# Two transformer layers on one core: expert rows weighted where they are made, and gathers that add

## The chip, the cores and the metric

The kernel runs on one core of a Trainium2 chip. The core has a matrix engine (TensorE, PE in the profile), three engines for element-wise work (VectorE or DVE, ScalarE or ACT, GpSimd or POOL), and a queue for transfers on SyncE (SP); POOL issues the transfers whose addresses come from a table of indices ("indirect" DMAs). The metric is the device time of one execution in microseconds (us).

## The reference, cut to what matters

The input x has 8 x 256 = 2048 tokens of 512 float32 values. Layer 1 is a linear attention of 32 heads plus, on the same normed input, a mixture of experts; layer 2 is a softmax attention plus a low-rank mixture.

```python
# layer 1
xn = layernorm(x)
x = x + linear_attention(xn) + ffn0(xn)
# ffn0: 2 of 16 experts for each token, and a shared one
def step(y, p):
    w1, b1, w2, b2, w3, b3, ge = p            # ge: this expert's gate of each token (0 if not chosen)
    h = silu(xt @ w1 + b1) * (xt @ w2 + b2)
    return (y + ge[:, None] * (h @ w3 + b3), None)
# layer 2
xn = layernorm(x)
x = x + attention(xn) + ffn1(xn)
# ffn1: 16 of 64 rank-16 factors for each token, gates G
h   = einsum('nd,krd->nkr', xf, A)
out = einsum('nkr,kdr->nd', h * G[:, :, None], B) * 2
```

Each token has two expert rows; the sum over experts is gate 1 x row 1 + gate 2 x row 2.

## The kernel before, in words

*Tiles and chunks.* The tokens form 4 chunks of 512, each of 4 tiles of 128 tokens. Large matrix products are done by a seven-product scheme of the Strassen kind in two-by-two blocks: products p1, p2, p6, p7, p5, p3, p4 go to PSUM banks `ps_a`, `ps_b`, `ps_e`, and the element-wise engines combine them.

*Layer 1.* A plan runs over two halves (of two chunks each), eight groups of four heads, two parts of a group and seven products (L1025). Other work is put between these products in small pieces: `later(after, f)` (L1030) notes a piece with the slot from which it may go, and `slot()` (L1034) runs those that are due after each product. Among them are:

- Routing: `scatter` (L1484 to 1492), 32 times. POOL makes a tile `token` with the token numbers (an iota, L1487) and scatters it by an indirect DMA (L1488) into a table with one line per expert slot. `read_table` (L1494) loads the table back, and `take_table` copies its first column to `whose`, the token of each slot.
- Experts: the class `Expert` (L1040 on), for 36 tiles of 128 slots in this run. Its construction gathers the tokens' rows and the weights (L1051, L1056, both into a tile `xw`: `xe` holds the rows, `we` the weights). `turn` transposes the rows (L1065) and copies them (L1067); `bias` then gathers the bias rows b3 into the same place `xe` (L1071); `up` makes h (L1083 to 1091); `down` multiplies with w3 (L1095), adds `xe` with DVE (L1100, shown at the helper's L103 as `ye`) and stores the row to `yd` in HBM (L1101). `expert(j)` (L1461) puts turn, bias, up and down at slots 10, 11, 14 and 22 after its start.
- At the end of the half: `wrapped_up` (L1564) makes chunk 0 ready for layer 2.

*From the experts' rows to x.* `gather` (L748 to 756) fetches for each tile and each of the two choices n the rows of `yd` by indirect DMA into a buffer `y`; `settle` (L758 to 767) is a DVE step, x = y * gate + x (L763). `finish` (L783) adds the attention's output, x = acc * rms + x (L789).

*The first factor.* `fa` has 14 pieces of 128 x 512 (seven products, two contraction halves). `load_part` (L937) loads pieces 0 to 8 in three calls during layer 1, each call three pieces into a tile that has room for 3.5 of them; `rest`, pieces 9 to 13, is loaded at the start of layer 2 (L1758), behind `wo` and `bo` (L1741, L1742). Piece 9 is the second half of product p5.

*Layer 2.* The chunk loop (L1778 on) does for every chunk i: the first low-rank product (L1806) as two half products, `low_rank(0, fill1)` and `low_rank(2, fill2)`, each by `seven` (L1692); attention in between; then the second product (L1913) and the stores (L1928). `seven` runs the lists `fill[k]` behind product k. Outputs of the first half product are multiplied by the gates on POOL and those of the second on DVE; both write `hg` out of a bank or a copy `cp` and a gate tile `spread_g`, loaded by SP (L920) into one of two buffers named `spread`. Chunk 0's first pair of gate tiles has room of its own. A half product has four outputs, written after p2, p5, p3 and p4; the first and third read one gate tile, the second and fourth the other. `fill2` holds `attended` (L1856): a POOL addition of `bo`, a product with `wo` (L1859) and a DVE addition.

In chunk i the input of chunk i + 1 is made ready: `next_x` loads x (L1772), the eight gathers stand ahead of everything else (L1862 to 1866), the settling steps in `fill1[3]`, `fill1[4]`, `fill2[2]`, `fill2[7]`, for i above 0 the `finish` steps in `fill1[2]` and `fill1[7]`, the norm's statistics in `fill2[7]`, `fill2[5]`, and its scaling in `fill2[3]`, `fill2[4]`. On POOL the parts of the attention's sums are also combined (`combine`, seven additions named `acc`).

*Order.* From the beginning of the chunk loop the instructions of ACT, POOL and DVE stand in the order in which the program gives them. TensorE's and SP's order is chosen by a scheduler. Every engine and SP work through their own queue in order, so an instruction that waits holds up all behind it.

Of the kernel before, what the change touches and what calls it, by code (L numbers as in the profile page):

```python
# [9 lines left out]
FP = mybir.dt.float32  # L10
# [63 lines left out]
def block_kernel(  # L74
# [566 lines left out]
    own_ = const.tile([P, NMT], I32, name="own_")  # L641
    whose = [const.tile([P, n], I32, name=f"whose{n}") for n in (READ, NMT - READ)]

    places = const.tile([P, TOP, NTT], I32, name="places")
# [103 lines left out]
    def gather(i, n, y, ts=range(TPC)):  # L748

        for t in ts:  # L750
            at = i * TPC + t
            nc.gpsimd.indirect_dma_start(
                out=y[:, t, :], out_offset=None, in_=yd[:, :],
                in_offset=bass.IndirectOffsetOnAxis(ap=slots[:, n, at : at + 1], axis=0),
                bounds_check=NSLOT - 1, oob_is_err=False,
            )

    def settle(i, n, x_, y, ts=range(TPC)):  # L758

        for t in ts:  # L760
            gate = slot_gates[:, n, i * TPC + t : i * TPC + t + 1]
            tc.keep_in_program_order(
                nc.vector.scalar_tensor_tensor(  # L763
                    x_[:, t, :], y[:, t, :], gate, x_[:, t, :], ALU.mult, ALU.add
                )
            )
# [160 lines left out]
    def load_fa(t, lo, hi):  # L927

        for n in range(lo, hi):
            p, c = list(WA)[n // 2], n % 2  # L930
            a = dict(
                p1=fa[:, 0], p2=fa[:, 1], p4=fa[:, 2], p7=low[0][:, 0], p5=low[0][:, 1], p6=low[0][:, 2], p3=low[0][:, 3]
            )[p]
            nc.sync.dma_start(out=t[:, n - lo], in_=a[:, bass.ts(c, C)])
            WA[p].append(t[:, n - lo])

    def load_part(n):  # L937

        t = toks.tile([P, 7, S], FP, tag="X", name="fa")
        load_fa(t.rearrange("p b n -> p (b n)")[:, 0 : 3 * C].rearrange("p (c k) -> p c k", c=3), 3 * n, 3 * n + 3)  # L940

# [3 lines left out]
    with in_order, tc.tile_pool(name="attn", bufs=1) as attn:  # L945
# [88 lines left out]
        def slot():  # L1034

            now[0] += 1
            n = 0
            while pieces and pieces[0][0] <= now[0] and n < (2 if len(pieces) > 12 else 1):
                f = pieces.pop(0)[2]
                f()  # L1040
                n += getattr(f, "func", f).__name__ not in ("add_a", "bias_sum", "silu", "bias", "gate", "fill_tile", "read_table", "take_table", "scatter", "load_sum", "sums1", "sums2", "sums3", "sums4", "settle0", "settle1", "out_sum", "load_sums", "store_sum", "combine", "finish", "store", "ranks", "tiles_of", "starts", "owners", "owned", "rows", "slots_of", "end", "placed", "chosen_at", "gated_at")


        class Expert:
# [24 lines left out]
            def bias(self):  # L1069
# [404 lines left out]
        def beyond():  # L1474

            with tc.If(n_used[0] > USUAL):  # L1476
                for j in range(USUAL, NMT):
                    e = Expert(j)
                    e.turn()
                    e.bias()  # L1480
                    e.up()
# [12 lines left out]
        def read_table(n=0):  # L1494
# [10 lines left out]
            def take_table():  # L1505
                tc.keep_in_program_order(
                    nc.vector.tensor_copy(
                        whose[n], rows.bitcast(I32).rearrange("p (j o) -> p j o", o=SAME)[:, :, 0]
                    )
                )  # L1510
                if n == 0:
                    read_table(1)
# [42 lines left out]

        def settled_in(i, x_, y):

            tc.keep_in_program_order(nc.sync.dma_start(out=x_, in_=xs_[i]))
            gathered(i, 0, y, 0)
            later(19, partial(settle, i, 0, x_, y))  # L1560
            gathered(i, 1, y, 20)
            later(39, partial(settle, i, 1, x_, y))

        def wrapped_up():  # L1564

            x_, y = spare8(), spare8()
            settled_in(0, x_, y)
            accs.append(x_)
# [171 lines left out]
    wo_t, bo_t = wob[:, 0, :], wob[:, 1, :]  # L1740
    nc.sync.dma_start(out=wo_t, in_=wo)  # L1741
    nc.sync.dma_start(out=bo_t, in_=bo.to_broadcast([P, C]))  # L1742
    HK = KR // 2
# [34 lines left out]
    for i in range(NCH):  # L1778
# [15 lines left out]
        def low_rank(j, fill):  # L1794
# [8 lines left out]
            def product(bank, w, xx, first):  # L1803
                for n in range(2):
                    for c in range(HC):
                        mm(  # L1806
                            bank[:, bass.ts(n, S)], w[c][:, bass.ts(j + n, P)], xx[:, c, :],
                            start=(first and n == 0 and c == 0), stop=(c == HC - 1),
# [64 lines left out]
        if following:  # L1873
# [156 lines left out]
```

## Time and profile before

| | |
|---|---|
| time, median of 3 runs | 2644.53 us (2644.34 to 2647.04) |
| profiled execution | 2642.12 us, of which span 2640.4 us |
| mean granted TensorE clock | 0.999 |
| TensorE busy | 2612.6 us, 99% |
| DVE busy | 1755.3 us, 66% |
| POOL busy | 1322.1 us, 50% |
| ACT busy | 704.3 us, 27% |
| settling steps (L763), DVE | 32, 27.6 + 10.5 us |
| gathers (L752), POOL | 32, 35.1 us |
| layer 2, chunk loop | from about 2359 us to the end |

A row of a timeline reads: start, time until the last of the row ends, engine, line, operation, output<-inputs, shape, count, and in square brackets the idle time of the engine before it with the instruction that ended it. A row of the waits reads: who waited for whom, total, number of times, longest (us). A row of the stretches reads: length, busy time (and count) of PE, PEld, DVE, ACT and POOL, then the granted TensorE clock, the share of the DMA engines and GB/s. Times are us from the span's start. Many additions share L103, a helper; they are told apart by the names of their tiles.

### The profile page before, as it was taken

The page shows a single profiled execution, that of the slowest core. Times are in us where ns is not written, and L with a number is a line of the kernel's source. Part 1 is how long each engine was busy: PE and PEld are TensorE (multiplying, and loading weights), DVE is VectorE, ACT ScalarE, POOL GpSimd, SP SyncE. Part 2 cuts the span into 40 slices and gives each one's busy share as a digit, 9 for nine tenths or more (in the row PEclk, how much of TensorE's full clock was granted, in tenths as well). Part 3 has the DMA queues.
Part 4 walks back from the last instruction along what each step waited for, and adds up shares of the span by engine and source line. Part 5 has one row for each costly group of instructions (what it writes and reads, how often), then busy time and mean ns, then how long its engine had stood idle before and what let it go on. Part 6 is the DMA issues. An engine that isn't in the chain of part 4 may idle for free. (4 is left out here: it accounts for less than half of the span.)

```text
span 2640.4 us, 38395 instructions
## 1 busy us (share of the span) xinstructions
PE 2612.6 (99%) x14250; PEld 2288.8 (87%) x14250; DVE 1755.3 (66%) x3211; ACT 704.3 (27%) x995; POOL 1322.1 (50%) x1297
## 2 busy tenths in 40 slices
PE   9999999999999999999999999999999999999999
PEld 6588888888888898989889898988989898977777
DVE  6795768686867686757456565656566565756774
ACT  5123232323232323232323122222312232321111
POOL 6756575656565656554534334352433453344411
PEclk9999999999999999999999999999999999999999
DMA  8996868686878777777777676777767686634201
GB/s 318 340 346 248 303 243 306 242 309 241 308 256 295 261 287 259 285 272 273 266 252 272 233 290 210 283 250 265 262 244 273 238 313 227 220 120 148 79 33 60
DMA packets 163117, 655.60 MB, mean 248 GB/s; under 512 B 19776, under 2 KB 22336, under 8 KB 160960
## 3 DMA queue, kind: packets, MB, share of 16 engines
q1 hardware_dynamic: 125504, 496.02, 53.0%
q10 hardware_dynamic: 21456, 95.95, 9.2%
q0 software_dynamic: 15968, 61.13, 6.9%
q8 instruction: 116, 1.90, 0.3%
q14 instruction: 73, 0.60, 0.1%
HBM read 512.13 MB, written 143.78 MB: 248 GB/s over the span
## 5 line engine op out<-in xcount | busy, mean ns | idle before, releaser
L1025 PE MATMUL ps_a<-xt,w 128*128 128x256 f32 x2688 | 712.6, 380 | 4.8 <-DVE c L103 4.7
L1025 PEld LDWEIGHTS ps_a<-xt,w 128*128 128x128 f32 x2688 | 470.1, 191 | 59.8 <-issue 9.3
L103 POOL TENSOR_TENSOR c<-c,r 128x512 f32<-128x512 f32 x256 | 323.2, 1286 | 247.3 <-DVE r L103 245.5
L1222 PE MATMUL ps_sc<-wo,gT 128*128 128x256 f32 x1792 | 422.4, 379 | 0.5 <-PEq L1476 0.5
L1222 PEld LDWEIGHTS ps_sc<-wo,gT 128*128 128x128 f32 x1792 | 334.3, 190 | 45.0 <-issue 2.3
L1025 PE MATMUL ps_e<-xt,w 128*128 128x256 f32 x1344 | 365.4, 381 | 3.7 <-PE ps_a L1025 3.0
L103 POOL TENSOR_TENSOR w<-w 128x512 f32<-128x512 f32 (+1 forms) x243 | 244.5, 1017 | 234.1 <-DVE w L103 194.8
L103 POOL TENSOR_TENSOR sums<-sums,sq 128x256 f32<-128x256 f32 x240 | 179.0, 746 | 313.9 <-ACT sq L1160 303.8
L1025 PEld LDWEIGHTS ps_a<-w,xt 128*128 128x128 f32 x1792 | 270.5, 191 | 23.0
L1025 PE MATMUL ps_a<-w,xt 128*128 128x128 f32 x1792 | 272.2, 274 | 0.0
L1025 PEld LDWEIGHTS ps_e<-xt,w 128*128 128x128 f32 x1344 | 230.2, 191 | 28.1 <-PE ps_a L1025 5.2
L103 DVE TENSOR_TENSOR acc<-ps_sc,acc 128x512 f32<-128x512 f32 x196 | 135.0, 689 | 153.0 <-PE ps_sc L1222 152.5
L1362 ACT COPY cp<-ps_a 128x512 f32<-128x512 f32 x160 | 93.5, 585 | 533.6 <-PE ps_a L1025 515.0
L103 DVE TENSOR_TENSOR cp<-ps_a,c 128x512 f32<-128x512 f32 x288 | 198.0, 687 | 54.1 <-PE ps_a L1025 45.7
L1169 DVE SCALAR_TENSOR_TENSOR gT<-ps_o,nw,c 128x256 f32<-128x256 f32 x256 | 112.1, 479 | 165.8 <-ACT sq L1160 139.0
L1160 ACT ACTIVATE sq<-ps_o 128x512 f32<-128x512 f32 x128 | 76.5, 597 | 485.0 <-PE ps_o L1150 445.7
L103 DVE TENSOR_TENSOR c<-ps_a,c 128x512 f32<-128x512 f32 x224 | 150.8, 684 | 76.8 <-PE ps_a L1025 75.8
L103 DVE TENSOR_TENSOR w<-w 128x256 f32<-128x256 f32 x333 | 179.1, 538 | 18.3 <-POOL w L103 14.5
L1025 PE MATMUL ps_b<-xt,w 128*128 128x256 f32 x672 | 181.9, 380 | 0.0
L103 DVE TENSOR_TENSOR s<-ps_sc,decay 128x384 f32<-128x384 f32 x256 | 141.3, 554 | 59.6 <-PE ps_sc L1137 58.1
L103 POOL TENSOR_TENSOR gT<-gT 128x512 f32<-128x512 f32 x128 | 164.8, 1288 | 5.8 <-DVE gT L1169 3.2
L1149 PE MATMUL ps_o<-s,c 128*128 128x256 f32 x512 | 154.4, 383 | 0.5
(304 smaller groups left out, 4130.1 us busy)
## 6 DMA issues: line engine op xcount, KB each, us to landing
xt<-xc SPq DMA_DIRECT2D x224, 896.0 KB
w<-in_w_att_dram SPq DMA_DIRECT2D x144, 512.0 KB
w<-in_w_att_dram SPq DMA_DIRECT2D x48, 384.0 KB
wo<-in_w_out_dram SPq DMA_DIRECT2D x56, 256.0 KB
decay<-dec SPq DMA_DIRECT2D x32, 384.0 KB
yd<-ye SPq DMA_DIRECT2D x36, 256.0 KB
wos<-wo ACTq DMA_DIRECT2D x32, 256.0 KB
wo<-wos SPq DMA_DIRECT2D x32, 256.0 KB
```

Of the source, the lines that this page charges most:

```text
L103: (eng or nc.vector).tensor_tensor(o, a, b, op)
L1025: mm(o, a, b, start=(first and ty == 0), stop=True, skip_group_check=True)
L1149: mm(po[:, bass.ts(hh, S)], v[:, 0:P], s[:, 0:S], start=True, stop=False)
L1160: nc.scalar.activation(sq, po, AF.Square)
L1169: nc.vector.scalar_tensor_tensor(gT[:, h, :], po[:, bass.ts(h, S)], nw[:, n : n + 1], self.c[:, 2 * h + t, 0:S], ALU.mult, ALU.mult,)
L1222: mm(py[:, bass.ts(t, S)], self.O[l, p][:, hh, bass.ts(t, P)], self.wo[p][:, hh, :], start=(t == 0 and hh == 0), stop=(hh == 1), skip_grou ...
L1362: nc.scalar.copy(c, bank)
```

## The change

1. The gate of a token is scattered with the token's number: POOL copies it into column 1 of `token`, 32 times, and `take_table` also copies that column, to `gate_of`.
2. A new step `weigh`, at slot 20 of an expert, multiplies the bias rows by the gate on ACT, and `down` computes ye = h w3 * gate + xe in one DVE step.
3. The gathers add to x where it lies (`compute_op`); `settle` is gone. They have no bounds check. A tile's second gather comes after its first has landed.
4. In the chunk loop the gathers of choice 0 stand in `fill1[1]` and those of choice 1 in `fill1[5]`. `finish` moves from `fill1[2]`, `fill1[7]` to `fill2[2]`, `fill2[7]`. In POOL's queue of layer 2, a chunk's gathers of choice 1 stand between the second and the third `hg`; the first four gathers of all stand ahead of the last `sums` steps of layer 1's attention.
5. `load_part(0)` and `load_part(1)` load one more half piece each (piece 9, in the room left in their tiles). `rest` has 4 pieces and is loaded ahead of `wo` and `bo`.

```diff
             nc.gpsimd.indirect_dma_start(
                 out=y[:, t, :], out_offset=None, in_=yd[:, :],
                 in_offset=bass.IndirectOffsetOnAxis(ap=slots[:, n, at : at + 1], axis=0),
-                bounds_check=NSLOT - 1, oob_is_err=False,
-            )
-
-    def settle(i, n, x_, y, ts=range(TPC)):
-
-        for t in ts:
-            gate = slot_gates[:, n, i * TPC + t : i * TPC + t + 1]
-            tc.keep_in_program_order(
-                nc.vector.scalar_tensor_tensor(
-                    x_[:, t, :], y[:, t, :], gate, x_[:, t, :], ALU.mult, ALU.add
-                )
+                compute_op=ALU.add,
             )
...
-            WA[p].append(t[:, n - lo])
+            WA[p].append([t[:, n - lo, bass.ts(m, P)] for m in range(4)])
+
+    split = []
...
+        t = toks.tile([P, 7, S], FP, tag="X", name="fa").rearrange("p b n -> p (b n)")
+        load_fa(t[:, 0 : 3 * C].rearrange("p (c k) -> p c k", c=3), 3 * n, 3 * n + 3)
+        if n < 2:
+            rest = t[:, 3 * C :]
+            nc.sync.dma_start(out=rest, in_=low[0][:, 1, C + n * S : C + (n + 1) * S])
+            split.extend(rest[:, bass.ts(m, P)] for m in range(2))
+        else:
+            WA["p5"].append(split)
...
+            def weigh(self):
+
+                j = self.j
+                self.gate = gate_of[j // READ][:, j % READ : j % READ + 1]
+                nc.scalar.activation(self.xe, self.xe, AF.Copy, scale=self.gate)
...
-                add(ye, py, self.xe)
+                nc.vector.scalar_tensor_tensor(ye, py, self.gate, self.xe, ALU.mult, ALU.add)
...
+            later(20, e.weigh)
...
+            nc.gpsimd.tensor_copy(token[:, 1:2].bitcast(FP), slot_gates[:, n, t : t + 1])
...
-        def settled_in(i, x_, y):
+        def settled_in(i, x_):
 
             tc.keep_in_program_order(nc.sync.dma_start(out=x_, in_=xs_[i]))
-            gathered(i, 0, y, 0)
-            later(19, partial(settle, i, 0, x_, y))
-            gathered(i, 1, y, 20)
-            later(39, partial(settle, i, 1, x_, y))
+            for n in range(TOP):
+                gathered(i, n, x_, 10 + 12 * n)
...
-    rest = work.tile([P, 5, C], FP, tag="fa", name="fa", bufs=1)
-    load_fa(rest, 9, 14)
+    rest = work.tile([P, 4, C], FP, tag="fa", name="fa", bufs=1)
+    load_fa(rest, 10, 14)
+    nc.sync.dma_start(out=wo_t, in_=wo)
+    nc.sync.dma_start(out=bo_t, in_=bo.to_broadcast([P, C]))
...
-            following = [next_x(i + 1), spare(), spare()]
-            for n in range(TOP):
-                gather(i + 1, n, following[1 + n])
+            following = [next_x(i + 1)]
...
+            for k, n in ((1, 0), (5, 1)):
+                fill1[k].append(partial(gather, i + 1, n, following[0]))
             if i:
-                for k, ns in ((2, (0, 1)), (7, (2, 3))):
-                    fill1[k].append(lambda ns=ns: finish(i + 1, following[0], ns, tc.keep_in_program_order))
-            for n, fill, k, ts in (
-                (0, fill1, 3, (0, 1)), (0, fill1, 4, (2, 3)), (1, fill2, 2, (0, 1)), (1, fill2, 7, (2, 3)),
-            ):
-                fill[k].append(partial(settle, i + 1, n, following[0], following[1 + n], ts))
+                for ns, k in (((0, 1), 2), ((2, 3), 7)):
+                    fill2[k].append(lambda ns=ns: finish(i + 1, following[0], ns, tc.keep_in_program_order))
```

More of the change, by code (lines that the diff above doesn't have):

```diff
@@ L642, in block_kernel @@
     whose = [const.tile([P, n], I32, name=f"whose{n}") for n in (READ, NMT - READ)]
+    gate_of = [const.tile([P, n], FP, name=f"gate_of{n}") for n in (READ, NMT - READ)]
     places = const.tile([P, TOP, NTT], I32, name="places")
@@ L934, in load_fa @@
             nc.sync.dma_start(out=t[:, n - lo], in_=a[:, bass.ts(c, C)])
-            WA[p].append(t[:, n - lo])
+            WA[p].append([t[:, n - lo, bass.ts(m, P)] for m in range(4)])
+    split = []
     def load_part(n):
-        t = toks.tile([P, 7, S], FP, tag="X", name="fa")
-        load_fa(t.rearrange("p b n -> p (b n)")[:, 0 : 3 * C].rearrange("p (c k) -> p c k", c=3), 3 * n, 3 * n + 3)
+        t = toks.tile([P, 7, S], FP, tag="X", name="fa").rearrange("p b n -> p (b n)")
[6 more added lines that the diff above has]
+            WA["p5"].append(split)
     def spare8():
@@ L1040, in slot @@
                 f()
-                n += getattr(f, "func", f).__name__ not in ("add_a", "bias_sum", "silu", "bias", "gate", "fill_tile", "read_table", "take_table", "scatter", "load_sum", "sums1", "sums2", "sums3", "sums4", "settle0", "settle1", "out_sum", "load_sums", "store_sum", "combine", "finish", "store", "ranks", "tiles_of", "starts", "owners", "owned", "rows", "slots_of", "end", "placed", "chosen_at", "gated_at")
+                n += getattr(f, "func", f).__name__ not in ("add_a", "bias_sum", "silu", "bias", "gate", "fill_tile", "read_table", "take_table", "scatter", "load_sum", "sums1", "sums2", "sums3", "sums4", "settle0", "settle1", "out_sum", "load_sums", "store_sum", "combine", "finish", "store", "ranks", "tiles_of", "starts", "owners", "owned", "rows", "slots_of", "end", "weigh", "placed", "chosen_at", "gated_at")
         class Expert:
@@ L1480, in beyond @@
                     e.bias()
+                    e.weigh()
                     e.up()
@@ L1505, in take_table @@
             def take_table():
[L1506 to L1510, printed above, removed]
+                at = rows.rearrange("p (j o) -> p j o", o=SAME)
+                for o, i in ((whose[n].bitcast(FP), 0), (gate_of[n], 1)):
+                    tc.keep_in_program_order(nc.vector.tensor_copy(o, at[:, :, i]))
                 if n == 0:
@@ L1554, in gathered @@
                 later(after + 2 * t, partial(gather, i, n, y, (t,)))
[L1556 removed]
+        def settled_in(i, x_):
             tc.keep_in_program_order(nc.sync.dma_start(out=x_, in_=xs_[i]))
[L1559 to L1562 removed]
+            for n in range(TOP):
+                gathered(i, n, x_, 10 + 12 * n)
         def wrapped_up():
             x_, y = spare8(), spare8()
[L1567 removed]
+            settled_in(0, x_)
             accs.append(x_)
@@ L1740, in block_kernel @@
     wo_t, bo_t = wob[:, 0, :], wob[:, 1, :]
-    nc.sync.dma_start(out=wo_t, in_=wo)
-    nc.sync.dma_start(out=bo_t, in_=bo.to_broadcast([P, C]))
     HK = KR // 2
@@ L1806, in product @@
                         mm(
-                            bank[:, bass.ts(n, S)], w[c][:, bass.ts(j + n, P)], xx[:, c, :],
+                            bank[:, bass.ts(n, S)], w[c][j + n], xx[:, c, :],
                             start=(first and n == 0 and c == 0), stop=(c == HC - 1),
```

## The prediction

> **What bounds the kernel now.** I read the engine table first, then the chain of waits of TensorE, then the table of stretches around every wait found, then the timelines there.
>
> ```profile
> PE 2612.6 (99%) x14250; PEld 2288.8 (87%) x14250; DVE 1755.3 (66%) x3211; ACT 704.3 (27%) x995; POOL 1322.1 (50%) x1297
> ...
> PE ps_e L1806 <- DVE cp L103: 5.1, 2, 4.1
> ...
> PE ps_a L1806 <- DMA fa<-low: 1.5, 1, 1.5
> PE ps_e L1913 <- DVE hg L103: 1.3, 2, 0.7
> ...
> 2380.00:2390.00 10.00, 6.21 (x23) 3.79 (x21) 9.84 (x12) 0.59 (x1) 9.77 (x7) 1.00 0.92 307
> 2390.00:2400.00 10.00, 9.66 (x45) 8.28 (x46) 9.46 (x18) 1.16 (x3) 7.67 (x8) 0.83 0.55 174
> ```
>
> TensorE is the bound: 2612.6 of 2640.4 us. Saved DVE work is worth only the TensorE waits that it ends. Waits this change can end lie in layer 2: 1.5 on a piece of the first factor, 4.1 and 0.99 on DVE's `cp`, 1.3 on DVE's `hg`. The last two rows show the 4.1 (6.21 of 10 us busy) and its echo: the granted clock is 0.83 in the next 10 us, 0.17 x 10 = 1.7 us of matmul time. All of it is under 10 us. About 0.2% (5.3 us) is what a measurement of this kernel can tell from no change.
>
> Chunk 0, DVE:
>
> ```profile
> 2369.29 5.04 DVE L763 SCALAR_TENSOR_TENSOR spare<-spare,slot_gates 128x512 f32<-128x512 f32 x2
> 2374.86 2.41 DVE L763 SCALAR_TENSOR_TENSOR spare<-spare,slot_gates 128x512 f32<-128x512 f32 x2
> 2380.10 1.31 DVE L103 TENSOR_TENSOR hg<-cp,spread_g 128x512 f32<-128x512 f32 x1 [2.22 <-DMA spread_g<-gd]
> 2381.93 2.83 DVE L763 SCALAR_TENSOR_TENSOR spare<-spare,slot_gates 128x512 f32<-128x512 f32 x2
> 2385.28 2.82 DVE L763 SCALAR_TENSOR_TENSOR spare<-spare,slot_gates 128x512 f32<-128x512 f32 x2
> 2389.63 0.66 DVE L103 TENSOR_TENSOR cp<-ps_e,cp 128x512 f32<-128x512 f32 x1
> ```
>
> The last row releases the waiting matmul; two pairs of settling steps stand between it and the `hg` of 2380.10. Now the same product in chunk 1, on POOL, the SP queue, DVE and TensorE:
>
> ```profile
> 2445.56 1.71 POOL L103 TENSOR_TENSOR hg<-cp,spread_g 128x512 f32<-128x512 f32 x1 [3.91 <-DVE cp L103]
> 2447.51 1.44 POOL L103 TENSOR_TENSOR hg<-cp,spread_g 128x512 f32<-128x512 f32 x1 [0.24 <-ACT cp L1817]
> ...
> 2448.97 4.17 SPq L920 DMA_DIRECT2D spread_g<-gd  x4
> ...
> 2454.01 1.36 DVE L103 TENSOR_TENSOR hg<-cp,spread_g 128x512 f32<-128x512 f32 x1 [0.36 <-DMA spread_g<-gd]
> ...
> 2463.61 0.66 DVE L103 TENSOR_TENSOR cp<-ps_e,cp 128x512 f32<-128x512 f32 x1
> ...
> 2464.32 1.99 PE L1806 MATMUL ps_e<-t,fa 128*128 128x256 f32 x8 [0.99 <-DVE cp L103]
> ```
>
> This is a chain without slack. The third POOL `hg` ends at 2448.95 and frees a `spread` buffer; SP reloads it from 2448.97; DVE's first `hg` of the second half product waits for that load; the `cp` add queues behind that `hg`; TensorE waits for the add. Chunk 2 has it too, with DVE waiting 0.74 us:
>
> ```profile
> 2527.90 0.97 DVE L103 TENSOR_TENSOR hg<-cp,spread_g 128x512 f32<-128x512 f32 x1 [0.74 <-DMA spread_g<-gd]
> ...
> 2536.68 1.89 PE L1806 MATMUL ps_e<-t,fa 128*128 128x256 f32 x8
> ```
>
> **The change part by part.**
>
> *Layer 1: token copies, weighing, STT in place of the add.* 32 POOL copies of one column: nearest row the 143 ns iota (L1487) on the same tile, 32 x 0.15 = 5 us, in a stage where POOL waits 318.4 us in all for `sq`. 36 ACT passes of 128x512: 0.585 us each by the ACT copies of `ps_a` (L1362), 21 us; ACT idles 533.6 us ahead of those 160 copies, 3.3 us each, so a pass fits between two. If each held up a PSUM copy TensorE needs, 21 us would be lost; that is the upper end. The weighing waits for the bias gather, issued nine slots earlier; gather to `ye` add is 14.6 us or more now (last gather 2041.3, last add 2055.9). `ye` grows from 0.69 to 0.74 us (the L789 median), behind the same wait. All taken as 0: bounds 0 and 21, much nearer 0.
>
> *Settling.* 32 DVE steps go, 38.1 us by their two groups (27.6 + 10.5). The 8 in attention hid behind TensorE: 0.
>
> *The half piece of `fa`.* The 1.46 us wait at 2366.47 goes. The four pieces left are issued ahead of `wo`, `bo`, at 2358.88 rather than 2359.74, and are needed at about 2367; the first piece took until 2366.47 from 2359.74, 6.7 us, so they land by about 2366. I take 1.2 of the 1.46 (bounds 0.5 and 1.46). `wo` and `bo` move back 1.7 us; first needed at 2375.57.
>
> *Chunk 0.* The eight gathers leave the front. Four go to about 2321; four stand after the second POOL `hg`. `hg` stays at 2380.10 at worst (its load isn't released by POOL in this chunk). Then on DVE: two `attended` adds, two stats pairs (2 x 0.80) and the `cp` add, back to back with starts 0.6 apart: 2380.10 + 1.23 + 1.2 + 1.6 + 0.66 = 2384.8. TensorE arrives at 2386.21 - 1.2 = 2385.0. So the 4.13 goes, the 1.7 of clock with it, and the 0.15 at 2419.59. What is late next: in the new order two groups of transposes (L296) stand directly behind each other and wait for DVE's scaling, and L816 comes straight after the last matmuls, waiting for a copy. A DVE step of 0.5 to 0.7 with its hand-over, twice: bounds 0 and 2.1, taken 1.5. Chunk 0: -(1.2 + 4.13 + 1.7 + 0.15) + 1.5 = **-5.7**.
>
> *Attention's end.* The first four gathers now stand on POOL ahead of its last `sums`, and wait for the 1 MB load issued at 2315.74, whose packets end at 2322.99 in the trace.
>
> ```profile
> 2323.84 1.53 POOL L103 TENSOR_TENSOR sums<-sums,sq 128x256 f32<-128x256 f32 x2 [3.32 <-ACT sq L1160]
> ...
> 2329.84 0.41 DVE L103 TENSOR_TENSOR head<-ps_sc,wsm 128x256 f32<-128x256 f32 x1
> ...
> 2330.40 3.67 PE L808 MATMUL ps_sc<-yT,wsm 128*128 128x512 f32 x8
> ...
> L752 POOL DMA_INDIRECT spare<-yd,slots x32: 994/1000/1745, 2216.9 to 2478.6; - x32
> ```
>
> A gather takes 1.0 us and the next starts 1.3 after it. So POOL runs 2323.0 + 5.2 = 2328.2 before `sums`, which end at 2329.8. `sq` has one buffer: ACT's next `sq` (0.6) ends at 2330.5, DVE's `gT`, now at 2328.85, starts then, and the `head` copies queued behind it end at 2331.9 instead of 2330.25. L808 follows them by 0.15 now: **+1.6**. Bounds: 0 (load in at 2320.4, where the DMA share falls off) and 3.
>
> *Chunks 1 and 2.* The second four gathers stand between the second and third POOL `hg`: the second ends at 2447.27, four gathers run to 2452.5, and the third `hg` starts there instead of 2447.51: 5.0 later. So are buffer, load and DVE's `hg` (2459.0). Behind it four settling steps (2 x 2.83) go, but four `finish` steps come into the same places: the same operation and shape, 0.74 alone, 1.41 each beside POOL's adds as the settling steps show there. So the add moves by 5.0 in chunk 1, by 2.9 if finishing costs 0.74: **+5.0** (bounds 2.9 and 6). In chunk 2 the add ends at 2536.35, 0.33 before TensorE starts: 5.0 - 0.3 = **+4.7** (bounds 4 and 5.7). The other DVE and POOL steps, `bo` adds included, end ahead of that `hg`.
>
> *Clock.* TensorE's gaps there become 0.99 + 5.0 = 6.0 and 4.7 us. The one gap of such size (4.13) cost 1.7 of clock; the slow stretch gives DVE the time that the 0.75 wait of `hg` takes now: 1.7 - 0.8 = 0.9 each, **+1.8** (bounds 0 and 3.4).
>
> The Trainium skill, "TensorE: Matmul & The Clock Gate" (Part 1), lets the clock fall only after an idle window of about 3.4 us in a grid that runs freely. By that page 6.0 us holds a whole window in about three phases of four, and 4.7 in about two of five; the term would be an estimated 1.0 and the whole sum 0.8 lower.
>
> *Waits between gathers.* Each second gather waits for the first's landing, some 45 us back by the order of issue: 0. "DMA: Bandwidth & Descriptors" (Rules for kernel authors) asks for that wait, which speaks against gathers that add: they cannot be issued eight in a row without it. How fast the adding transfer lands, no row shows. Plain gathers land in 3 to 4 us in quiet stretches, in 14 in the crowded one (issued 2369.04, landed 2383.08). In chunks 1 and 2 `finish` comes over 7 us after the last issue. In chunk 0 the first stats come about 8 us after it, where 14 would cost 4 to 6. I take 0.
>
> Sum: -5.7 + 1.6 + 5.0 + 4.7 + 1.8 = **+7.4 us**. The profiled execution took 2642.12 us, 2.4 under the runs' median of 2644.53: 2649.5 there, 2652 as a median, +0.28%.
>
> **Rivals.**
> *A, faster:* the gathers without a bounds check take POOL far less. If they hold it under 0.3 us each, `sums` and reload are late by less than DVE can make up, and the -5.7 stands alone: 2644.5 - 5.7 = 2639. For it: the settling on the path of the wait does go. Against: every indirect transfer of the trace, whatever it moves, takes 0.99 to 1.02.
> *B, slower still:* adding transfers land at the crowded 14 us in chunk 0; the stats wait on DVE ahead of the `cp` add, and 4 us come back: 2656. For it: DMA share 0.90 to 1.04 there. Against: half of the gathers left that stretch.
> *C, no difference:* delays shorter than reckoned: `finish` at 0.74 (+2.9), chunk 2 at 4, no clock drop, attention 0: -5.7 + 2.9 + 4.0 = +1.2, 2645.7. For it: POOL and DVE shift against each other.
>
> **How the numbers follow.** Forecast 0.60, A 0.12, B 0.13, C 0.15. Range 2642 to 2658: it leaves out A and takes in C, B with 2 us to spare, and the bounds added (2652 + 6). Faster 0.12; within 0.2% (2639.2 to 2649.8) 0.16; slower 0.72, forecast and B.
>
> **What would show it.** Right: the 4.13 and 1.46 waits gone; TensorE waiting 4 to 6 us for `cp` before L1806 in chunks 1 and 2, behind a DVE `hg` waiting 5 us for `spread_g`, behind four gathers between the POOL `hg`s; a gap of 1 to 2 us before L808. Wrong: gathers at well under 1 us on POOL, the reload issued at its old distance from the third `hg`'s matmuls, ACT late in the expert stage, or DVE waiting for gathers in chunk 0.

## The result and the profile after

The changed kernel takes 2668.51 us (median of six runs, 2667.37 to 2671.07), the kernel before 2645.45 us in the same session (2644.07 to 2647.87): a ratio of 1.0088, interval 1.0075 to 1.0101. It is slower by 23 us, where 7 were forecast. The profiled execution took 2670.56 us with a span of 2668.6, against 2642.12 and 2640.4 before: 28.2 us of span to explain.

The engine table of after, the same five figures as before:

```profile
PE 2623.6 (98%) x14250; PEld 2296.4 (86%) x14250; DVE 1731.9 (65%) x3181; ACT 725.7 (27%) x1031; POOL 1336.8 (50%) x1329
```

TensorE does the same 14250 matmuls, but is busy for 11.0 us more (2623.6 against 2612.6): 9.6 of them go with the clock, since 22.6 us of its work fell into stretches at half clock, against 3.4 before, and half of the difference is lost. The other 17.2 us of the span are idle time (45.0 against 27.8). DVE lost 23 us of work, and none of it came back as time.

What TensorE waited for, from the table of waits of after (who waited for whom, total, times, longest):

```profile
PE ps_e L1810 <- DVE cp L103: 11.6, 3, 6.9
PE ps_a L1024 <- DVE c L103: 6.9, 8, 1.3
PE ps_sc L799 <- DVE head L103: 4.2, 1, 4.2
PE ps_sc L296 <- DVE spare L280: 3.8, 3, 2.4
...
PE ps_sc L1863 <- DVE spare L103: 2.7, 1, 2.7
```

The wait of 1.5 us for a piece of `fa` is gone. The wait of 4.1 us for `cp` in chunk 0 is gone too, but the same row now holds two longer ones, 6.89 in chunk 1 and 4.31 in chunk 2, and three rows (L799, L296, L1863) are new. L1024 in layer 1 had 4.7 us before.

Stretches of after around these waits, 10 us each (busy time and count of PE, PEld, DVE, ACT, POOL; then the granted clock, the DMA share and GB/s). The first three stand at the end of attention and behind chunk 0's waits, the last two in chunk 1:

```profile
2330.00:2340.00 10.00, 5.85 (x20) 3.90 (x19) 3.40 (x13) 2.23 (x3) 9.15 (x10) 0.78 0.65 98
2340.00:2350.00 10.00, 10.00 (x30) 5.65 (x29) 5.14 (x25) 1.42 (x4) 0.68 (x1) 0.88 0.00 0
...
2400.00:2410.00 10.00, 6.20 (x23) 4.92 (x24) 9.93 (x12) 2.14 (x3) 9.02 (x6) 0.69 0.37 56
...
2470.00:2480.00 10.00, 3.49 (x11) 1.74 (x10) 8.78 (x7) 1.34 (x2) 9.76 (x7) 0.78 0.15 57
2480.00:2490.00 10.00, 6.96 (x18) 5.63 (x19) 9.43 (x20) 0.30 (x1) 8.13 (x6) 0.54 0.50 71
```

Where TensorE is idle, POOL or DVE is nearly full, and the clock is below 1 in the same rows or in the row behind. In the 20 us of the last two rows TensorE works 10.45 us.

Since both kernels run the same matmuls in nearly the same order, the time of the matmul of the same number in both traces shows where the loss arises. The table gives how far after lags behind before, by stage. The forecast has its clock term (0.9 each) in chunks 1 and 2.

| stage | lag at its end, us | made in the stage | forecast |
|---|---|---|---|
| start of the program, to 217 us | 0.8 | +0.8 | 0 |
| layer 1's routing, 217 to 1031 us | 3.8 | +3.0 | 0 |
| rest of layer 1's experts, to 2263 us | 3.4 | -0.4 | 0 |
| attention's end, to 2359 us | 9.6 | +6.2 | +1.6 |
| chunk 0, to 2455 us | 9.6 | 0.0 | -5.7 |
| chunk 1, to 2488 us | 20.5 | +10.9 | +5.9 |
| chunk 2, to the end | 27.8 | +7.3 | +5.6 |

The timelines (start, time until the last of the row ends, engine, line, operation; in brackets the idle time before, and what ended it) show each stage. Attention's end, after: the last of the first four gathers, POOL's `sums`, ACT's `sq`, DVE's `head` and the product that waits for it:

```profile
2332.31 1.55 POOL L753 DMA_INDIRECT spare<-yd,slots  x1 [0.31 <-issue]
2333.29 2.13 POOL L103 TENSOR_TENSOR sums<-sums,sq 128x256 f32<-128x256 f32 x2
...
2335.45 0.60 ACT L1165 ACTIVATE sq<-ps_o 128x512 f32<-128x512 f32 x1 [8.68 <-POOL sums L103]
...
2337.07 0.41 DVE L103 TENSOR_TENSOR head<-ps_sc,wsm 128x256 f32<-128x256 f32 x1
...
2337.63 6.03 PE L799 MATMUL ps_sc<-yT,wsm 128*128 128x512 f32 x8 [4.15 <-DVE head L103]
```

The four gathers start at 2326.73, 2328.59, 2330.45 and 2332.31, one every 1.86 us.

Chunk 0, after:

```profile
2384.49 0.69 DVE L103 TENSOR_TENSOR hg<-cp,spread_g 128x512 f32<-128x512 f32 x1
2390.38 0.69 DVE L103 TENSOR_TENSOR spare<-ps_sc,spare 128x512 f32<-128x512 f32 x1 [5.20 <-POOL spare L103]
...
2384.67 1.92 POOL L753 DMA_INDIRECT spare<-yd,slots  x1 [0.30 <-issue]
2388.48 5.52 POOL L103 TENSOR_TENSOR spare<-spare,wob 128x512 f32<-128x512 f32 x4
...
2400.84 2.88 DVE L280 TENSOR_SCALAR spare<-spare,mv,rstd 128x512 f32<-128x512 f32 x2
...
2394.53 1.99 PE L1810 MATMUL ps_e<-t,fa 128*128 128x256 f32 x8 [0.40 <-DVE cp L103]
2402.38 0.66 PE L296 MATMUL ps_sc<-ident,spare 128*128 128x128 f32 x4 [2.40 <-DVE spare L280]
```

The matmul that lost 4.13 us waits 0.40 now. But POOL's additions of `bo` stand behind the gathers, DVE waits 5.20 us for them, and its scaling (L280) reaches TensorE late.

Chunk 1, after:

```profile
2456.60 1.55 POOL L753 DMA_INDIRECT x<-yd,slots  x1
...
2462.19 1.54 POOL L753 DMA_INDIRECT x<-yd,slots  x1 [0.30 <-issue]
2463.18 3.07 POOL L103 TENSOR_TENSOR hg<-cp,spread_g 128x512 f32<-128x512 f32 x2
2465.63 5.50 POOL L103 TENSOR_TENSOR spare<-spare,wob 128x512 f32<-128x512 f32 x4
...
2465.06 2.53 SPq L911 DMA_DIRECT2D spread_g<-gd  x4
...
2471.22 2.90 DVE L103 TENSOR_TENSOR hg<-cp,spread_g 128x512 f32<-128x512 f32 x1 [7.94 <-DMA spread_g<-gd]
...
2482.33 0.66 DVE L103 TENSOR_TENSOR cp<-ps_e,cp 128x512 f32<-128x512 f32 x1
...
2474.77 1.39 PE L1863 MATMUL ps_sc<-wob,oT 128*128 128x512 f32 x2 [2.67 <-DVE spare L103]
2483.04 3.78 PE L1810 MATMUL ps_e<-t,fa 128*128 128x256 f32 x8 [6.89 <-DVE cp L103]
```

This is the forecast chain: gathers, third `hg`, reload, DVE's `hg`, `cp`, TensorE. The gathers, the reload and DVE's `hg` each take longer than I had reckoned, and the chain ends in two waits, 2.67 and 6.89. In chunk 2 it is the load alone:

```profile
2555.93 0.69 DVE L103 TENSOR_TENSOR hg<-cp,spread_g 128x512 f32<-128x512 f32 x1 [8.29 <-DMA spread_g<-gd]
...
2562.72 3.78 PE L1810 MATMUL ps_e<-t,fa 128*128 128x256 f32 x8 [4.31 <-DVE cp L103]
```

### The profile page after: what moved, and what is told of

Read it like the earlier page. It is cut to its first block, busy times and chain, and to the rows that moved or that the text cites. A ratio compares the mean times of both kernels' runs of the same rounds, so it can differ in the third digit from the quotient of the medians.

```text
span 2668.6 us, 38369 instructions
## 1 busy us (share of the span) xinstructions
PE 2623.6 (98%) x14250; PEld 2296.4 (86%) x14250; DVE 1731.9 (65%) x3181; ACT 725.7 (27%) x1031; POOL 1336.8 (50%) x1329
## 5 line engine op out<-in xcount | busy, mean ns | idle before, releaser
L1024 PE MATMUL ps_a<-xt,w 128*128 128x256 f32 x2688 | 712.7, 380 | 6.9 <-DVE c L103 6.9
L1024 PEld LDWEIGHTS ps_a<-xt,w 128*128 128x128 f32 x2688 | 470.5, 191 | 61.9 <-DVE c L103 9.9
L1024 PE MATMUL ps_e<-xt,w 128*128 128x256 f32 x1344 | 365.6, 381 | 3.5 <-PE ps_a L1024 3.0
L1024 PEld LDWEIGHTS ps_a<-w,xt 128*128 128x128 f32 x1792 | 270.4, 191 | 23.0
L1024 PE MATMUL ps_a<-w,xt 128*128 128x128 f32 x1792 | 272.2, 274 | 0.0
L1024 PEld LDWEIGHTS ps_e<-xt,w 128*128 128x128 f32 x1344 | 230.3, 191 | 28.6 <-PE ps_a L1024 5.6
L103 DVE TENSOR_TENSOR w<-w 128x256 f32<-128x256 f32 x333 | 181.9, 546 | 18.2 <-POOL w L103 14.4
L1024 PE MATMUL ps_b<-xt,w 128*128 128x256 f32 x672 | 181.9, 380 | 0.0
```

Source lines behind the costliest of these rows:

```text
L103: (eng or nc.vector).tensor_tensor(o, a, b, op)
L1024: mm(o, a, b, start=(first and ty == 0), stop=True, skip_group_check=True)
```

## The experiments

The theory after the result: the losses of chunks 1 and 2 come from the gathers' place between POOL's second and third `hg`; that of attention's end from the four ahead of `sums`; chunk 0's gain is taken back by gathers ahead of the `bo` additions. The rival to all three was that the additions of the new gathers, not their place, make the loss. The profiled executions differ by up to 4.8 us in their first 130 us, ahead of the first scatter, so stages are compared by matmul number where a few us matter.

### e1_early: the gathers of choice 1 in another place, chunks 1 and 2

```diff
-            for k, n in ((1, 0), (5, 1)):
+            for k, n in ((1, 0), (1 if i else 5, 1)):
```

> In chunks 1 and 2 the gathers of choice 1 move up behind those of choice 0, into the long idle stretch of POOL ahead of its first hg; everything else is the changed kernel. If the place of these gathers is the cause (POOL late with its third hg, reload of spread_g late, DVE's hg and the cp behind it late): TensorE's waits of 2.7 + 6.9 us in chunk 1 and 0.8 + 4.3 us in chunk 2 fall to about 1 us together, the clock stays up there, and of the 25 us lost after chunk 0's second product begins some 19 come back: about 2649. If the cause is the finish steps that now stand on DVE ahead of the cp: the waits fall by less than half, and the time is above 2658.

Measured: 2651.15 us, ratio 1.0021 (1.0011 to 1.0031). The waits of TensorE:

```profile
PE ps_sc L296 <- DVE spare L280: 3.8, 3, 2.4
PE ps_sc L799 <- DVE head L103: 3.5, 1, 3.5
...
PE ps_e L1810 <- DVE cp L103: 1.7, 2, 1.3
```

Two of the three `cp` waits are gone (11.6 us to 1.7 in all) and so is the 2.7 at L1863; the other two rows stay. The lag does not grow any more in chunks 1 and 2 (6.2 to 5.8 us), where after lost 18.2. The place is the cause there: the median is 17 us lower. (By matmul number attention's end also lost 3 us less here, with no drop of the clock behind a wait of 3.5; nothing was moved there.)

### e2_plain: gathers that do not add

```diff
-                compute_op=ALU.add,
```

> The gathers of the changed kernel, in their new places, without the addition (they overwrite x, so two terms of the sum are left out). If the addition is what makes a gather longer on POOL (1.56 us and 0.30 to the next, against 1.00 and 0.30): a gather takes 1.0 again, the third hg is 2.2 us earlier in chunks 1 and 2 and the waits there fall by about that each, as does the one before L799 at attention's end; 2656 to 2662. If the missing bounds check or the place is what makes it longer: 1.56 stays and the time is that of the changed kernel within 2 us.

Measured: 2657.34 us, ratio 1.0046 (1.0029 to 1.0064). The group of the 24 gathers into `spare` (minimum/median/maximum ns of one), after first, then without the addition:

```profile
L753 POOL DMA_INDIRECT spare<-yd,slots x24: 1542/1556/1924, 2236.2 to 2546.6; - x24
```

```profile
L753 POOL DMA_INDIRECT spare<-yd,slots x24: 942/948/1162, 2239.1 to 2536.0; - x24
```

The addition costs POOL 0.61 us a gather. The 0.05 that remain to the 1.00 of before may be the dropped bounds check; no run parts that from the new place. Without the addition the wait at L799 is gone, but 7.1 us for `cp` remain in chunk 1, where I expected some 2 less: DVE's `hg` waits 4.93 us for its load in place of 7.94, but then takes 3.55 in place of 2.90. So the price matters at attention's end, and the place alone is enough in chunk 1.

### e3_weigh and e4_fa: parts of the change on the kernel before

The first has parts 1 and 2, with a plain addition left in the settling step:

```diff
-                nc.vector.scalar_tensor_tensor(
-                    x_[:, t, :], y[:, t, :], gate, x_[:, t, :], ALU.mult, ALU.add
-                )
+                nc.vector.tensor_tensor(x_[:, t, :], y[:, t, :], x_[:, t, :], ALU.add)
...
+            nc.gpsimd.tensor_copy(token[:, 1:2].bitcast(FP), slot_gates[:, n, t : t + 1])
```

> The kernel before with the first two parts alone: gate scattered with the token, expert rows weighted on ACT and in the STT; the settling steps stay as plain additions, gathers and first factor as before. The changed kernel's trace shows 2 to 3 us more TensorE waiting before 1240 us. If the 32 POOL copies are its cause: 2 to 3 us slower than before (2647 to 2648.5) with the same waits at L1025. If the weighing on ACT costs something, the loss lies between 1240 and 2060 us. If neither: no change.

Measured: 2647.1 us, ratio 1.0008 (0.9998 to 1.0017). As a time it is no difference, but its lag grows from 2.9 to 5.8 us between 217 and 1031 us, as in after, and by nothing from 1235 to 2060, where only the weighing goes on. So weighing on ACT is free, and the 3.0 us fall into the time of the token copies, which run to 861 us (e10_marks, below, takes the copies away). Its row beside that of before (the 4.7):

```profile
PE ps_a L1023 <- DVE c L103: 6.4, 8, 1.1
```

The second has part 5:

```diff
-    rest = work.tile([P, 5, C], FP, tag="fa", name="fa", bufs=1)
-    load_fa(rest, 9, 14)
+    rest = work.tile([P, 4, C], FP, tag="fa", name="fa", bufs=1)
+    load_fa(rest, 10, 14)
```

> The kernel before with the last part alone: one more piece of the first factor loaded in attention, four pieces left and loaded ahead of wo and bo. If the 1.46 us wait before the second half of p5 simply goes: 2644.0, 1.2 to 1.5 us less. If the product that follows waits for its own piece or DVE for spread_g instead, no change; TensorE's wait of 4.1 us for cp in chunk 0 then grows by what the first loses.

Measured: 2647.53 us, ratio 1.0004 (0.9994 to 1.0014), which tells nothing of 1.4 us. By matmul number the lag falls from 3.1 to 1.65 us at that place, and the wait for `fa` is gone, while 4.2 us for `cp` stay. The part does what it says.

### e5_late: also the first chunk's gathers later

On e1_early. POOL's gathers for chunk 1 stand behind copies of results that are made late in attention, so they run after the product that was late:

```diff
+            for n in range(TOP):
+                if i == 0:
+                    late = (head.G[:, 0, 0:1], head.probs[0][:, 0, 0:1])[n]
+                    seen = small.tile([P, 1], FP, tag="seen", name="seen")
+                    tc.keep_in_program_order(nc.gpsimd.tensor_copy(seen, late))
+                    gather(1, n, following[0])
+                else:
+                    fill1[1].append(partial(gather, i + 1, n, following[0]))
```

> On top of e1_early: the gathers into chunk 1's input wait on POOL for a late result of attention (a one-column copy of the gates G ahead of choice 0, of the softmax ahead of choice 1), so that none stands ahead of attention's last sums and none between POOL's hg steps. If they cause the 3 to 4 us wait before L799 and chunk 0's waits of the transposes (2.4, 0.75, 0.67 us): the first goes whole, the second by more than half, and the drop of the clock behind it too; 3.1 + 5 us less than e1_early, 2643 to 2644. If chunk 0's waits come from DVE beside POOL's combining additions only, they stay, and it is 2648.

Measured: 2641.9 us, ratio 0.9992 (0.9983 to 1.0001). No wait at L799; the lag falls in chunk 0 from 4.9 to -0.5 us, 5.4 us of gain. What I had forecast for chunk 0 (-5.7) was there to be had, with the gathers out of the way. One `cp` wait is left, of 1.3 us.

### e6_finish: finish steps back in the first half product

```diff
-                    fill2[k].append(lambda ns=ns: finish(i + 1, following[0], ns, tc.keep_in_program_order))
+                    fill1[k].append(lambda ns=ns: finish(i + 1, following[0], ns, tc.keep_in_program_order))
```

> On top of e5_late: the finish steps back in the first half product of chunks 1 and 2 (their gathers have landed there by then). Takes four DVE steps of 0.74 to 1.41 us from the path of chunk 1's cp: its wait of 1.3 us goes, 0.5 in chunk 2 at most; 1 to 1.8 us less than e5_late, 2641 to 2643. If the wait comes from the reload of spread_g, no change.

Measured: 2639.65 us, ratio 0.9982 (0.9973 to 0.9991). The 1.3 is gone, so it came from the four `finish` steps among `attended`. At the end it is 5.6 us ahead of before, with the 3 us of the token copies still in it.

### e7_tokens: the token copies on ACT

On e6_finish: the token tiles are made eight slots ahead of their scatter, and ACT copies the gate.

```diff
-            nc.gpsimd.tensor_copy(token[:, 1:2].bitcast(FP), slot_gates[:, n, t : t + 1])
+            nc.scalar.copy(token[:, 1:2].bitcast(FP), slot_gates[:, n, t : t + 1])
...
+                        later(12 * (e - 3 * at) + 52, partial(mark, e // TOP, e % TOP))
```

> On top of e6_finish: the token numbers are made eight slots ahead of their scatter, and the gate is copied in by ACT instead of POOL. If the 3.0 us that layer 1 loses up to 1000 us (in steps of about 0.6, also with the first two parts alone) come from POOL's copy ahead of the scatter: 3 us less than e6_finish, 2638 to 2640, which is 0.2% under the kernel before. If they come from the order of POOL's other additions beside DVE's: less than 1.5 us.

Measured: 2650.68 us, ratio 1.0022 (1.0013 to 1.0032): a miss. ACT's copies wait for POOL, whose iota stands behind other work, and ACT's PSUM copies queue behind them until TensorE waits:

```profile
ACT token L1497 <- POOL token L1496: 158.5, 28, 9.6
```

```profile
PE ps_a L1024 <- ACT cp L1367: 10.0, 5, 2.3
```

14.5 us are lost by 1031 us, with three drops of the clock among them. A wait moved to an engine with much idle time can still be dear when that engine feeds TensorE from a queue.

### e10_marks: all token tiles made once

On e6_finish: two iotas and one copy ahead of the first scatter write all token numbers and gates, and a table line has 2 words in place of 16.

```diff
-SAME = 16
+SAME = 2
...
+            if t == n == 0:
+                for m in range(TOP):
+                    nc.gpsimd.iota(marks[:, m], pattern=[[P, NTT], [0, SAME]], base=0, channel_multiplier=1)
+                nc.gpsimd.tensor_copy(marks[:, :, :, 1].bitcast(FP), slot_gates)
+            token = marks[:, n, t, :]
```

> On top of e6_finish: all token numbers and gates are made at once, by two iotas and one copy ahead of the first scatter, in rows of 2 numbers in place of 16; the other 31 iotas and 31 copies are gone. If layer 1's 3.0 us come from POOL's work ahead of each scatter: they go, perhaps 0.5 more since the iotas go too, 2636 to 2637. If the order of POOL's other additions is the cause: less than 1.5 us, 2638 or more. Smaller rows could make the scatter and its load slower, which nothing waits for in the trace.

Measured: 2634.36 us (2634.12 to 2634.63), ratio 0.9958 (0.9944 to 0.9971). This version beats both kernels: 0.42% under before, 1.3% under the change as made. Its engine table and its longest wait of TensorE:

```profile
PE 2611.7 (99%) x14250; PEld 2289.2 (87%) x14250; DVE 1725.9 (66%) x3181; ACT 725.7 (28%) x1031; POOL 1329.9 (51%) x1270
```

```profile
PE ps_a L1025 <- DVE c L103: 4.1, 8, 1.3
```

POOL has 59 instructions fewer than in after; between 217 and 1031 us it gains 1.0 us on before, where after lost 3.0. The run changes two things at once, POOL's steps and the length of a table line, and does not part them. Of a span of 2632.4 us TensorE is busy 2611.7.

### e8_reload: a gate tile that need not be reloaded

Back to chunk 1: which link of the chain carries the loss? With four `spread` buffers (and one of `spare` given up for the room) the load no longer waits for the third `hg`.

```diff
-        return work.tile([P, TPC, C], FP, tag="spare", name="spare")
+        return work.tile([P, TPC, C], FP, tag="spare", name="spare", bufs=1)
...
-            return spread_into(work.tile([P, 2, CH], FP, tag="spread", name="spread_g"), i, j)
+            return spread_into(work.tile([P, 2, CH], FP, tag="spread", name="spread_g", bufs=4), i, j)
```

> The changed kernel with four buffers in place of two for spread_g (room from a second buffer of spare, which nothing needs at that time): the reload waits for no POOL hg, the order on POOL, ACT, DVE and TensorE is untouched. If the release of the buffer is the link between the gathers and DVE: DVE's waits of 8 us for spread_g go in chunks 1 and 2; then the bo additions, still late on POOL, set the pace, with 3 us of TensorE's wait left in chunk 1 and 1 in chunk 2; 2652 to 2656. If transfers that add slow the reload, or the finish steps and DVE's contention with POOL make the cp late: waits of over 6 and 3 us stay, above 2662.

Measured: 2667.42 us, ratio 1.009 (1.0075 to 1.0106). The theory of the reload fell: the load is in, and TensorE still waits 2.67 and 6.42 us. DVE and POOL in chunk 1:

```profile
2459.33 10.80 DVE L103 TENSOR_TENSOR hg<-cp,spread_g 128x512 f32<-128x512 f32 x1
```

```profile
2459.20 3.07 POOL L103 TENSOR_TENSOR hg<-cp,spread_g 128x512 f32<-128x512 f32 x2
2461.65 5.50 POOL L103 TENSOR_TENSOR spare<-spare,wob 128x512 f32<-128x512 f32 x4
2466.55 11.39 POOL L103 TENSOR_TENSOR acc<-acc 128x512 f32<-128x512 f32 x7
```

One multiplication of DVE, 0.69 us by itself, takes 10.80 us. Over all that time POOL works off, without a gap, what has queued up behind its gathers: two `hg`, four `bo` additions and the first two `acc`, each starting 1.22 us after the one before it. DVE's step ends 0.5 us after POOL begins the third `acc`, the first of them with idle time ahead of it (0.08 us). New theory: a DVE step with both inputs in SBUF is shut out as long as POOL's steps follow each other without a wait.

As it stands that is too wide. In e1_early POOL's four `bo` additions also follow each other 1.22 us apart without idle time, and DVE's `hg` comes through between them:

```profile
2457.65 5.41 POOL L103 TENSOR_TENSOR spare<-spare,wob 128x512 f32<-128x512 f32 x4
```

```profile
2460.43 1.51 DVE L103 TENSOR_TENSOR hg<-cp,spread_g 128x512 f32<-128x512 f32 x1 [0.55 <-DMA spread_g<-gd]
```

Over all thirteen traces the steps of DVE on 128x512 that take over 2.4 us stand beside a POOL run that began right behind gathers. So what is shown is narrower: such a run shuts DVE's step out.

### e9_pause and e11_both: pauses in POOL's queue

A pause is a POOL copy of one element per partition that reads the step's result, put behind each `hg` and each `bo` addition. e9_pause is e8_reload with pauses, e11_both is the changed kernel with pauses and its two buffers.

```diff
+        def pause(o):
+            seen = small.tile([P, 1], FP, tag="seen", name="seen")
+            tc.keep_in_program_order(nc.gpsimd.tensor_copy(seen, o))
...
+                    pause(o[:, 0, 0:1])
...
+            pause(xc[:, t, 0:1])
```

> e8_reload with a pause on POOL: after each of its hg multiplications and bo additions of layer 2 a one-element copy of the result, which waits for that result. In e8_reload DVE's hg no longer waits for its reload and yet takes 10.8 us in chunk 1, until POOL's run of eight multiplications and additions, each begun 0.6 us before the last one ends, comes to its first own wait. If such a run keeps a DVE step with two SBUF inputs out (lock-out): with pauses DVE's hg takes under 3 us, the waits of 2.7 + 6.4 us in chunk 1 fall to 4 or less in all, 4.3 in chunk 2 to 2 or less, and the clock stays up for longer: 2652 to 2660, although POOL has more to do. If something else makes that hg long: it stays near 10 us, and the time is that of e8_reload or more, 2667 to 2671.

Measured: 2663.16 us (2656.74 to 2666.09), ratio 1.0058 (1.0043 to 1.0074), 3 us above what I expected; this profiled execution was 4.8 us late at its start. In chunk 1:

```profile
2467.24 2.91 DVE L103 TENSOR_TENSOR hg<-cp,spread_g 128x512 f32<-128x512 f32 x1
2473.17 0.69 DVE L103 TENSOR_TENSOR spare<-ps_sc,spare 128x512 f32<-128x512 f32 x1 [3.02 <-POOL seen L1800]
```

```profile
2480.16 3.78 PE L1814 MATMUL ps_e<-t,fa 128*128 128x256 f32 x8 [3.27 <-DVE cp L103]
```

The step takes 2.91 us in place of 10.80, TensorE waits 3.27 in place of 6.42, and chunk 1 loses 4.8 us by matmul number in place of 10.6. That fits the lock-out. What is left has a third source: behind its `hg` DVE waits 3.02 us for POOL's first `bo` addition and the pause behind it (`seen`), late behind the gathers as in chunk 0. In chunk 2 the wait is 3.27 as well, where I expected 2 at most, and DVE waits the same 3.02 us there. How much of it is the pauses themselves no run shows.

> The changed kernel (two buffers for spread_g, so the reload waits for POOL's third hg again) with the pauses of e9_pause. If the reload, too, is late enough to matter by itself: DVE's hg in chunk 1 waits 6 to 8 us for spread_g and then takes under 2 us, TensorE waits 5 to 7 us there, against 3.3 with the early reload and 9.6 without pauses; 2664 to 2668. If the lock-out alone held DVE and the reload was in time: waits of 3 to 4 us as in e9_pause, and 2661 to 2664.

Measured: 2663.96 us (2663.66 to 2671.09), ratio 1.0083 (1.0065 to 1.01). In chunk 1:

```profile
2468.11 0.69 DVE L103 TENSOR_TENSOR hg<-cp,spread_g 128x512 f32<-128x512 f32 x1 [8.28 <-DMA spread_g<-gd]
```

```profile
2469.46 1.12 PE L1869 MATMUL ps_sc<-wob,oT 128*128 128x512 f32 x2 [0.80 <-DVE spare L103]
2476.86 3.35 PE L1814 MATMUL ps_e<-t,fa 128*128 128x256 f32 x7 [6.27 <-DVE cp L103]
```

With POOL pausing, the late load alone holds DVE for 8.28 us, and TensorE for 0.80 + 6.27 = 7.1. So in chunk 1 there are two links, and each is enough by itself: TensorE waits 9.6 us with both (2.67 + 6.89), 9.1 with the lock-out alone, 7.1 with the late load alone, 3.3 with neither, each by one profiled execution. (The pauses themselves put the load of e11_both 0.6 us later than in after.) To take one away shows little; that is why e8_reload looked like no effect.

## Why the prediction was wrong in size

Sign, places and chain were right: the 4.13 and the 1.46 went, TensorE waits for `cp` in chunks 1 and 2 behind a DVE `hg` that waits for `spread_g` behind four gathers, and there is a gap before L799. The sum was +7.4; the profile has +28.4. By its steps:

- *"A gather takes 1.0 us and the next starts 1.3 after it."* The row was of plain gathers. One that adds takes 1.56, the next starts 1.86 after it: +0.56 each, 2.2 us for every four. I wrote that no row showed how fast the adding transfer lands, and bounded that; its price on POOL I took from the plain one without a bound above. e2_plain puts the difference on the addition.
- *Attention's end, +1.6 (bounds 0 and 3).* The gap was 4.15 us. Of the +6.2, some 4.0 are the gap and 2.4 the clock, half rate from 2335.56 for 6.83 us, of which TensorE worked 4.8. No clock term stood there at all.
- *Chunk 0, -5.7.* "`hg` stays at 2380.10 at worst" and the end of both waits hold. The failed step is "two `attended` adds, ... back to back": POOL's `bo` additions, on which they depend, stand behind the four gathers, which I costed only for `hg`. DVE waits 5.20 us, the scaling comes late, TensorE waits 3.8 us at L296 (I had 1.5 for "what is late next") and the clock falls for 6.83 us. e5_late, without the gathers there, gained 5.4.
- *Chunk 1, "four gathers run to 2452.5 ... 5.0 later".* DVE's `hg` ended 9.1 us late, beyond the 9.6 by which the stage began late: the reload was issued 6.5 late, landed 6.04 us after its issue and not 4.96 (+1.1), and `hg` took 2.90 and not 1.36 (+1.5). The last term is the lock-out, which e8_reload shows can be far greater. I had taken it that POOL's steps would follow the gathers as they had stood, alternating with DVE's; instead they had queued up. The trace before held a sign of it: in the row "2369.29 5.04" that the prediction shows, the second settling step took 4.38 us, beside three `hg` steps of POOL that stood right behind its gathers:

```profile
2370.05 3.72 POOL L103 TENSOR_TENSOR hg<-cp,spread 128x512 f32<-128x512 f32 x3
```

`finish` at 1.41 each was right (2.82 a pair).
- *Chunk 2, +4.7.* The wait is 4.31; with the clock (6.83 us at half rate from 2560.84, TensorE working 4.95 of it, so 2.5) that makes 6.8 of the 7.3.
- *Clock, +1.8.* The 9.6 us at half clock are the largest miss. Before, the clock fell once while TensorE had work, for 3.41 us. After, it fell four times, for 6.83, 6.83, 13.65 and 6.83 us. I priced the gaps of chunks 1 and 2 like the one that I saw, and gave attention's end and chunk 0 no clock term. The clock's changes in the traces lie on a grid of 3.41 us; half rate lasts until a window of it has little idle time (0.13 of it or less here), and in chunk 1 a second gap fell into the slow stretch and kept it going.
- *"All taken as 0" in layer 1.* +3.0, inside my bounds of 0 and 21, but not where I looked: weighing on ACT is free (e3_weigh), the 32 copies cost (e3_weigh loses the same 2.9 there; e10_marks, with one copy, loses none). In the table of waits of POOL, the wait of the scatters for the tile's last write, before and after:

```profile
POOL table L1488 <- POOL token L1487: 8.9, 32, 0.3
```

```profile
POOL table L1496 <- POOL token L1495: 18.9, 32, 0.9
```

A copy holds POOL for 0.21 us in the mean, and the scatter waits 0.3 us longer for it: 16.6 us in all (6.6 + 10.0), of which 3.0 reach TensorE, 2.2 of them as waits for DVE's `c` (4.7 to 6.9).
- Taken at nothing, and so it is: the settling in attention, the serial waits between gathers, the weighing. Gathers were no wait of DVE in chunk 0, so rival B did not come about, though all of the 5.7 came back in chunk 0 by another way; rival A's condition, under 0.3 us, is refuted by 0.95 even without the addition.

The rule on the clock which the prediction weighed, in the Trainium skill, "TensorE: Matmul & The Clock Gate", Part 1, made the sum 0.8 lower; the runs go the other way, and here the measurement decides. Over the thirteen profiled executions, each drop of the clock in layer 2 stands behind a window of 3.41 us that was idle for 0.53 to all of its length, and not only behind a wholly idle one (after: 0.61, 0.80, 0.78, 0.71); windows idle for 0.52 or less had no drop behind them, and one of 0.56 had none. So a gap can cost different amounts by where it falls in the grid: at attention's end 4.15 us cost 6.83 of half rate in after and 4.21 us cost 3.41 in e9_pause; 3.47 us in e1_early, split over two windows, cost none.

## What to carry to other kernels

Before an instruction is put into an in-order queue, list everything behind it there, and price it by a row of the same operation; an added operation in a transfer (here the addition, +0.6 us each) is a new operation and wants a bound above. Where POOL's queue is held up by gathers, its held-up steps afterwards come without pauses, and a DVE step with two inputs in SBUF can then be shut out for longer than the delay itself (10.80 us in e8_reload, behind four gathers that held POOL for some 7). On a TensorE that is 99% busy the stretches of half clock count beside the gaps (9.6 us and 17.2 here): list the gaps over 1.8 us (an estimate: 0.53 of a window of 3.41), give each a bound of 7 us of half rate (one of the four in after lasted 13.65), and move work out of the way before counting what was saved.

## What the runs showed that I had not expected

- *Lock-out of DVE by a POOL queue.* 10.80 us in e8_reload for a step of 0.69, across POOL steps that started every 1.22 us. In the quiet order of e1_early the same step takes 1.51 beside POOL's additions, which start 1.22 us apart too. The Trainium skill, "SBUF — State Buffer", Who interferes with whom, says that a DVE step with two SBUF inputs contends with a GpSimd step that reads SBUF, and that issue order decides who blocks. The runs agree that DVE can be shut out, but for some eight POOL instructions begun one after another, not one. Why the steps behind gathers do this and the equally close ones of e1_early do not is open; the pauses of e9_pause show only that it ends with them.
- *The clock.* Half rate lasted 3.4 to 13.7 us after idle gaps of 2 to 10 us, 34.1 us in all in after.
- *The price of adding.* 1.56 us of POOL for a gather of 128 rows of 2 KB that adds, 0.95 for one that does not, neither with a bounds check.
- *Open.* Why the gate tile takes 6 us to land here in place of 5; how much of the 3.27 us left in chunks 1 and 2 of e9_pause is the pauses' own; what shifts the first 130 us from one execution to the next.
